# Four-layer transformer block on one core: order of the third layer's projections, weight loads on another queue, and accumulation banks by use

## The chip, the cores and the metric

One core of one Trainium2 chip runs the whole program. The metric is device time in microseconds (us), the median of three runs. The core's engines work in parallel, each through its own instruction stream in order: TensorE (PE; its weight loads are shown as PEld), VectorE (DVE), ScalarE (ACT), GpSimd (POOL) and SyncE (SP), which here only issues transfers. DMA transfers are issued by SP and by POOL, each in its own order, and are carried by 16 DMA engines. Matrix products land in PSUM, which here is cut into three score buffers of two banks each and two further banks for everything else. SBUF holds all other tiles.

## What is computed

x has the shape 4 x 1024 x 256 (batch, rows, width), float32. Four layers follow each other, each with a residual:

```python
x = x + attn_a(layernorm(x))     # layer 1: 16 heads of 64, full softmax attention
x = x + ffn(layernorm(x))        # layer 2: 256 -> 1024 -> 256, exact gelu
x = x + attn_b(layernorm(x))     # layer 3: the same attention from low-rank projections
x = x + ffn(layernorm(x))        # layer 4: the same weights as layer 2

# attn_b, with its own normalization inside (scale and bias), b, s, d = x.shape
c_q, c_kv = h @ w_down_q.T, h @ w_down_kv.T            # 256 -> 128
q, k, v   = c_q @ w_up_q.T, c_kv @ w_up_k.T, c_kv @ w_up_v.T
q, k      = rope(q), rope(k)                           # even and odd features rotated
attn      = softmax(q @ k.T / 8)
out       = (attn @ v) @ w_out.T + x_normalized        # attn_b adds its own input
```

## The kernel before

The order of every engine's work is written out by hand; no scheduler changes it. Instructions of one engine run in the order in which the program issues them, and a semaphore makes an instruction wait for what it reads or overwrites.

**Attention (`attention`, L163 to L323).** Heads are taken in pairs, because two heads of 64 fill the 128 rows of TensorE: 4 batches x 8 pairs = 32 pairs. A pair has eight steps, one for each 128 query rows: 256 steps in each of layers 1 and 3. Two steps are one block `h`. In step s the loop `steps_with` (L294) issues, in this order:

1. `invert(s)`: reciprocal of the softmax sums (DVE), copied into the probabilities (ACT).
2. `scores(s + 1)`: eight matmul records `sc` (L214), and `exponentials(s + 1, 0)`: the negated row maximum `nmax` (DVE, L224) and the exponential (ACT, L225) of the first head.
3. In even steps `send(s // 2 - 1)` on POOL (five of 16 transfers of a block, L261) and `project` of an earlier block: output projection `po` (PE), copy `got` (ACT, L290), residual add (POOL, L292).
4. `weigh(h, part)`: half of the weighted sums `av` (PE) of block h = (s - 4) // 2, first half in even steps, second in odd. The accumulation stays open from the even to the odd step.
5. `exponentials(s + 1, 1)` for the second head.
6. In odd steps `divide(h)`: `av` times the inverted sums gives `oT` (DVE, L275).
7. `turn(s)`: transposes 32 x 32 squares of the probabilities (DVE, L244).
8. In odd steps `send(s // 2)` on SP (the other eleven transfers): squares from `T` to `pT`, which completes the transpose. `weigh` reads `pT` about two and a half steps later.
9. The `pieces` that are due in step s: projections of the next pair and preparations of the next batch.

**The pieces.** In layer 1 (`pair_a`, L484) the next pair's `pq` (keys, queries: `qk`) and `pv` (`values`) come in odd steps. In layer 3 (`pair_b`, L578) too: `qk` in steps 7, 1, 3 and 5 (counted within a pair), `values` in steps 5 and 7, always at the end of the step. `qk` ends in a scaled copy (ACT) and two transfers on POOL that swap neighbouring features (`turned`, L598); `rotate`, one step later, is three POOL operations (L603 to L605). The three weights `w` of a pair come by POOL transfers in step 4 (L584), the output weight `wo` in step 7 (L190). A new batch in layer 3 (`batch_b`, L536) needs four transposes `tr` with their copies (`turned`, in odd steps), and four down projections `pc` (`down`, L562), two in each of two odd steps.

**Banks.** `ps_mm` (L52) has two buffers that are handed out in turn to `tr`, `pq`, `pv`, `pc`, `av` and `po`.

**Layer 2 and 4 (`ffn_between`, L393).** Blocks of 512 rows; layer 3's first batch and first pair are prepared inside layer 2.

**Start (L635 to L640).** Measuring and normalizing batch 0, its transposes, all four `pq` and four `pv` of the first pair, then the first scores.

Of the kernel before, what the change touches and what calls it, by code (L numbers as in the profile page):

```python
# [9 lines left out]
F32 = mybir.dt.float32  # L10
AF = mybir.ActivationFunctionType
ALU = mybir.AluOpType
# [19 lines left out]
SENT = NG * HB * NK * SQ  # L32
POOL_DMA = 5
EPS = 1e-5


@with_exitstack
def hybrid_block_kernel(
# [10 lines left out]
    small = ctx.enter_context(tc.tile_pool(name="small", bufs=6))  # L49

    ps_sc = ctx.enter_context(tc.tile_pool(name="ps_sc", bufs=3, space=PSUM))
    ps_mm = ctx.enter_context(tc.tile_pool(name="ps_mm", bufs=2, space=PSUM))  # L52


    pool = lambda name, bufs: ctx.enter_context(tc.tile_pool(name=name, bufs=bufs))
# [83 lines left out]

    def transposed(dst, src, c, affine=None):  # L140

        tr = ps_mm.tile([P, TQ, P], F32, tag="mm", name="tr")
        for t in range(TQ):
            nc.tensor.transpose(tr[:, t, :], src[:, t, ts(c, P)], ident)
        trf = tr.rearrange("p t q -> p (t q)")
        if affine is None:
            nc.scalar.copy(dst[:, c, :], trf)  # L147
        else:
            nc.scalar.activation(
                dst[:, c, :], trf, AF.Identity,  # L150
                scale=affine[0][:, c : c + 1], bias=affine[1][:, c : c + 1],
            )
# [7 lines left out]
                    start=(first and i == 0), stop=(last and i == len(parts) - 1),  # L160
                )

    def attention(prep_batch, prep_pair, wo):  # L163

# [20 lines left out]

        def load_out(g):
            wos[g] = wop.tile([P, D], F32, tag="wo", name="wo")
            nc.gpsimd.dma_start(wos[g], wo[ts(pairs[g][1], P), :])  # L190

        for g, (b, pr) in enumerate(pairs):
            for k, f in prep_batch(b) if pr == 0 else ():
# [69 lines left out]
        def weigh(h, part):  # L263
            v = tiles[HB * h // NT]["v"]()
            if part == 0:
                av[h] = ps_mm.tile([P, HB * P], F32, tag="mm", name="av")
            half = range(part * NT // 2, (part + 1) * NT // 2)
            paired(
                av[h], [(v[:, k], [pT[h][:, :, :, j * NT + k, :] for j in range(2)]) for k in half],
                first=(part == 0), last=(part == 1),  # L270
            )

        def divide(h):
            oT[h] = otp.tile([P, HB * P], F32, tag="oT", name="oT")
            nc.vector.tensor_tensor(  # L275
                oT[h].rearrange("p (q a i) -> p a q i", a=NG, i=SQ),
                av.pop(h).rearrange("p (a q i) -> p a q i", a=NG, i=SQ),
                pT.pop(h)[:, :, :, 2 * NT, :],
                op=ALU.mult,
            )  # L280

        def project(h):
            g, t0 = divmod(HB * h, NT)
            b, pr = pairs[g]
            po = ps_mm.tile([P, HB, D], F32, tag="mm", name="po")
            for t in range(HB):
                paired(po[:, t, :], [(oT[h][:, ts(t, P)], [wos[g]] * 2)])
            oT.pop(h)
            got = tmp.tile([P, HB, D], F32, tag="tmp", name="got")
            nc.scalar.copy(got, po)  # L290
            xd = xs[b][:, t0 : t0 + HB, :]
            nc.gpsimd.tensor_add(xd, xd, got)  # L292

        def steps_with(others):  # L294
            for k, f in others:
                pieces.setdefault(k, []).append(f)
            for s in range(-1, n + LAG + 1):
                h, part = divmod(s - LAG, HB)
                ahead = 0 <= s + 1 < n
                if 0 <= s < n:  # L300
                    invert(s)
                if ahead:
                    scores(s + 1)
                    exponentials(s + 1, 0)
                if part == 0 and 0 <= s // HB - 1 < n // HB:
                    send(s // HB - 1, nc.gpsimd, squares[len(squares) - POOL_DMA :])
                    T.pop(s // HB - 1)
                if part == 0 and 0 <= h - 1 < n // HB:
                    project(h - 1)
# [35 lines left out]
    def ffn(rows, store):  # L345
# [29 lines left out]
        def down(n, t):  # L375
            b, qb = blocks[n]
            if t % 2 == 0:
                po[n] = ps_mm.tile([P, 2, D], F32, tag="mm", name="po")
# [72 lines left out]
    def layer_a():  # L451
# [5 lines left out]
        def batch_a(b):  # L457
            work = []
            for qb in range(NQB):
                k = {}  # L460

                def straight(t, b=b, k=k, qb=qb):
                    if t == 0 and b == 0:
                        for i in range(TQ):
                            rows.measure(qb, i)
                        rows.finish[qb]()
                    if t == 0:
                        k["xn"] = xnp.tile([P, TQ, D], F32, tag="xn", name="xn")
                    standardize(
                        k["xn"][:, t, :], xs[b][:, qb * TQ + t, :],  # L470
                        *rows.factors(NQB * b + qb, t)[:2],
                    )

                def turned(c, b=b, k=k, qb=qb):
                    if c == 0:
                        p, tag = ((lowp, "low"), (highp, "high"))[qb]
                        hTs[b, qb] = p.tile([P, NC, QB], F32, tag=tag, name="hT")
                    transposed(hTs[b, qb], k["xn"], c)

                work += [(10 * qb + t, lambda t=t, f=straight: f(t)) for t in range(TQ)]  # L480
                work += [(10 * qb + 5 + 2 * c, lambda c=c, f=turned: f(c)) for c in range(NC)]
            return work

        def pair_a(b, pr):  # L484
# [9 lines left out]
            def qk(i, qb):  # L494
                name = ("qT", "kT")[i]
                if qb == 0:
                    made[name] = qkp.tile([P, S], F32, tag=name, name=name)
                pq = ps_mm.tile([P, QB], F32, tag="mm", name="pq")
# [9 lines left out]
            def values(m):  # L508
                if m == 0:
                    made["v"] = vp.tile([P, NT, P], F32, tag="v", name="v")  # L510
                pv = ps_mm.tile([P, 2, P], F32, tag="mm", name="pv")
# [12 lines left out]

        later = [(4 + i, lambda i=i: rows.measure(2 + i // TQ, i % TQ)) for i in range(6 * TQ)]
        later += [(4 + 6 * TQ, lambda: rows.finish[2]())]
        first, steps = attention(batch_a, pair_a, wo_a)
        return first, lambda others: steps(later + others)


    def layer_b(rows):
# [4 lines left out]
        def batch_b(b):  # L536
            work = []
            for qb in range(NQB):
# [23 lines left out]
                def down(i, k=k, qb=qb):  # L562
                    if qb == 0:
                        cs[b, i] = highp.tile([P, NC, QB], F32, tag="high", name=f"c{i}").rearrange(
                            "p c q -> p (c q)"
                        )
                    pc = ps_mm.tile([P, QB], F32, tag="mm", name="pc")
# [4 lines left out]
                work += [(10 * qb + t + 2, lambda t=t, f=second: f(t)) for t in range(TQ)]  # L572
                work += [(10 * qb + 7 + 2 * c, lambda c=c, f=turned: f(c)) for c in range(NC)]

                work += [(3 * NT + 1 - 2 * i, lambda i=i, f=down: f(i)) for i in range(2)]
            return work

        def pair_b(b, pr):  # L578
            made = {}

            def load():
                w = made["w"] = wp.tile([P, 3, NC, P], F32, tag="w", name="w")[:, :, 0, :]
                for i, up in enumerate((wuq, wuk, wuv)):
                    nc.gpsimd.dma_start(w[:, i], up[:, ts(pr, P)])  # L584

            def qk(i, qb):

                pq = ps_mm.tile([P, QB], F32, tag="mm", name="pq")
# [18 lines left out]
            def values(qb):  # L607
                if qb == 0:
                    made["v"] = vp.tile([P, NT, P], F32, tag="v", name="v")
                pv = ps_mm.tile([P, TQ, P], F32, tag="mm", name="pv")  # L610
# [90 lines left out]
```

## Time and profile before

| | us |
|---|---|
| median of three runs (lowest, highest) | 3390.42 (3387.98, 3392.9) |
| the profiled execution | 3386.3 |
| its span, first to last instruction | 3384.5 |
| first transpose to last transpose of layer 1 | 1435.6 |
| first transpose to last transpose of layer 3 | 1400.7 |

Busy time of the engines over the span: TensorE 3253.2 (96%), VectorE 2593.1 (77%), ScalarE 1902.1 (56%), GpSimd 1800.8 (53%). The span in 40 slices of 85 us each, one digit a slice (tenths busy; 9 is 90% or more), shows the four layers: slices 1 to 17 are layer 1, 18 to 20 layer 2, 21 to 37 layer 3, the rest layer 4.

```
PE   7999999999999999999999999999999999999999
DVE  6988888888888888951059998898889989999200
POOL 3333334343333333330258887888788978886200
DMA  7788788788887888840038888888888888888200
```

The transfers of `pT` are 2816 on SP (median 4.2 us from issue to landing) and 1280 on POOL (4.7 us), 136 KB each. The swapped copies `turned` are 256 on POOL, 128 KB each (median 2.7 and 3.0 us). In the views, `128*64` ahead of a shape is the part of TensorE's array that is used, and `x8` at a line's end counts merged instructions.

### The profile page before, as it was taken

To read this page: it belongs to the slowest core of one execution; us is meant where nothing else is said; L and a number is where in the kernel's file an instruction comes from. 1 tells how busy PE (TensorE), PEld (TensorE's weight loads), DVE (VectorE), ACT (ScalarE), POOL (GpSimd) and SP (SyncE) were. 2 spreads that over 40 slices of the span, in tenths; PEclk is the share of its full clock that TensorE was granted. 3 is DMA by queue.
4 is the path that set the end of the run, shared out by engine and by line. 5 is a ranking of instruction groups with operands and counts; after the bars stand their busy time and mean duration, and the time that the engine had idled before them with its cause. 6 is when DMAs were issued, how large, how long until landed. Compare 5 with 4: busy or idle time off the path is not lost.

```text
span 3384.5 us, 60980 instructions
## 1 busy us (share of the span) xinstructions
PE 3253.2 (96%) x20864; PEld 1679.4 (50%) x20864; DVE 2593.1 (77%) x2638; ACT 1902.1 (56%) x3667; POOL 1800.8 (53%) x2546
## 2 busy tenths in 40 slices
PE   7999999999999999999999999999999999999999
PEld 3445444544454444456554444444444444444566
DVE  6988888888888888951059998898889989999200
ACT  5566556655565555542445665566656655655332
POOL 3333334343333343330258887888788978886200
PEclk9999999999999999999999999999999999999999
DMA  7788788888887888840038888888888888888200
GB/s 211 204 210 208 205 214 212 211 208 214 210 210 206 214 214 210 210 115 3 6 105 233 227 239 226 237 246 231 224 236 243 242 225 239 243 235 228 61 19 19
DMA packets 229585, 647.36 MB, mean 191 GB/s; under 512 B 74304, under 2 KB 82496, under 8 KB 229280
## 3 DMA queue, kind: packets, MB, share of 16 engines
q1 hardware_dynamic: 143696, 400.74, 46.2%
q0 software_dynamic: 85584, 242.74, 25.2%
q8 instruction: 170, 2.79, 0.4%
q14 instruction: 135, 1.11, 0.1%
HBM read 35.00 MB, written 4.19 MB: 12 GB/s over the span
## 4 chain that ended last, share of the span: by engine, by line
PE 67%; DVE 11%; SPq 8%; DMA 6%; issue 4%; ACT 3%; POOL 1%; DVEq 0%; POOLq 0%; ACTq 0%
PE sc L214 19%; PE av L158 18%; SPq L261 8%; PE pq L158 8%; PE po L380 7%; PE ph L369 6%; DVE nmax L224 5%; DVE T L244 5%; DMA pT<-T 5%; PE po L158 4%; PE pv L158 4%; ACT p L225 1%; PE pc L158 1%; DMA turned<-qT 1%; DVE oT L275 1%
## 5 line engine op out<-in xcount | busy, mean ns | idle before, releaser
L225 ACT ACTIVATE p<-sc,nmax 128x1024 f32<-128x1024 f32 x1024 | 1143.8, 1117 | 729.5 <-DVE nmax L224 729.5
L224 DVE TENSOR_REDUCE nmax<-sc 128x1 f32<-128x1024 f32 x1024 | 1201.9, 1215 | 325.5 <-PE sc L214 324.9
L244 DVE STREAM_TRANSPOSE T<-p 128x2176 f32<-128x2176 f32 x512 | 1246.3, 2434 | 11.1 <-ACT p L233 3.9
L158 PE MATMUL av<-pT,v 128*64 128x256 f32 x8192 | 994.7, 385 | 79.4 <-DMA pT<-T 56.9
L214 PE MATMUL sc<-kT,qT 64*128 64x512 f32 x4096 | 1033.0, 617 | 7.2 <-ACT p L225 7.2
L261 POOL DMA_DIRECT2D pT<-T x1280 | 625.8, 496 | 777.9 <-issue 268.7
L158 PEld LDWEIGHTS av<-pT,v 128*64 128x64 f32 x8192 | 579.5, 137 | 542.9 <-issue 273.3
L214 PEld LDWEIGHTS sc<-kT,qT 64*128 64x128 f32 x4096 | 366.8, 187 | 483.9 <-issue 352.5
L292 POOL TENSOR_TENSOR x<-x,got 128x512 f32<-128x512 f32 x256 | 326.8, 1276 | 224.7 <-ACT got L290 220.4
L233 ACT COPY p<-total 128x128 f32<-128x128 f32 x512 | 152.0, 297 | 312.5 <-DVE total L232 312.4
L387 DVE TENSOR_TENSOR x<-x,po 128x512 f32<-128x512 f32 x32 | 21.9, 685 | 363.4 <-PE po L380 363.4
L158 PE MATMUL po<-wo,oT 128*64 128x256 f32 x2048 | 277.7, 392 | 0.4 <-DVE oT L275 0.4
L373 ACT ACTIVATE gT<-ph,b_sb 128x512 f32<-128x512 f32 x128 | 87.4, 685 | 305.4 <-PE ph L369 305.3
L158 PE MATMUL pq<-hT,w 128*64 128x512 f32 x1024 | 247.0, 605 | 5.1 <-DVE oT L275 4.0
L158 PEld LDWEIGHTS po<-wo,oT 128*64 128x64 f32 x2048 | 124.3, 136 | 230.2 <-issue 129.5
L380 PE MATMUL po<-w_sb,gT 128*128 128x256 f32 x1024 | 226.0, 381 | 6.2 <-ACT hT L147 6.2
L369 PE MATMUL ph<-hT,w_sb 128*128 128x512 f32 x512 | 228.9, 601 | 0.2 <-ACT hT L147 0.2
L380 PEld LDWEIGHTS po<-w_sb,gT 128*128 128x128 f32 x1024 | 193.5, 190 | 38.4 <-ACT hT L147 9.0
L225 ACT ACTIVATION_READ_ACCUMULATOR p<-sc,nmax 128x1 f32 x1024 | 201.4, 197 | 0.0
L355 POOL TENSOR_TENSOR x<-x,b_sb 128x256 f32<-128x256 f32 x64 | 44.5, 727 | 276.4 <-ACT xn L138 276.4
L604 POOL TENSOR_TENSOR turned<-turned,sin_sb 128x512 f32<-128x512 f32 x128 | 162.3, 1268 | 0.0
L369 PEld LDWEIGHTS ph<-hT,w_sb 128*128 128x128 f32 x512 | 97.0, 192 | 117.1 <-issue 111.3
(88 smaller groups left out, 2188.8 us busy)
## 6 DMA issues: line engine op xcount, KB each, us to landing
pT<-T SPq DMA_DIRECT2D x2816, 136.0 KB, 4.2
pT<-T POOLq DMA_DIRECT2D x1280, 136.0 KB, 4.7
turned<-kT POOLq DMA_DIRECT2D x128, 128.0 KB, 2.7
turned<-qT POOLq DMA_DIRECT2D x128, 128.0 KB, 3.0
w<-in_wqkv_a POOLq DMA_DIRECT2D x96, 128.0 KB, 4.9
wo<-in_wo_a POOLq DMA_DIRECT2D x32, 128.0 KB, 4.4
wo<-in_wo_b POOLq DMA_DIRECT2D x32, 128.0 KB, 3.4
out<-x SPq DMA_DIRECT2D x16, 256.0 KB, 2.1
```

The costliest lines, as they stand in the source:

```text
L158: nc.tensor.matmul(out[ts(j, DH)], lhsT[:, ts(j, DH)], rhs[j], start=(first and i == 0), stop=(last and i == len(parts) - 1),)
L214: nc.tensor.matmul(sc[s, j][:, ts(m, 512)], qT()[rows, ts(qs, P)], kT()[rows, ts(m, 512)], start=True, stop=True,)
L224: nc.vector.tensor_reduce(nmax, sc[s, j], AX.X, ALU.max, negate=True)
L225: nc.scalar.activation(probs[s][:, ts(j, NT)].rearrange("p k c i -> p (k c i)"), sc.pop((s, j)), AF.Exp, bias=nmax, accum_out=total[s][:, ...
L233: nc.scalar.copy(probs[s][:, 2 * NT].rearrange("p (j c) i -> p j (c i)", j=2), t.unsqueeze(2).to_broadcast([P, 2, DH]),)
L244: nc.vector.transpose(T[h][:, :, q, :, :].rearrange("p c k i -> p k c i"), probs.pop(s))
L261: engine.dma_start(pT[h][ts(c, SQ), a], T[h][ts(a, SQ), c])
L292: nc.gpsimd.tensor_add(xd, xd, got)
L369: nc.tensor.matmul(ph, w1_sb[:, c, ts(f, P)], hT[n][:, c, :], start=(c == 0), stop=(c == NC - 1),)
L373: nc.scalar.activation(gT[n][:, f, :], ph, AF.Gelu, bias=b1_sb[:, f : f + 1])
L380: nc.tensor.matmul(po[n][:, t % 2, :], gT[n][:, f, ts(t, P)], w2_sb[:, f, :], start=(f == 0), stop=(f == NF - 1),)
L604: nc.gpsimd.tensor_mul(turned, turned, sin_sb[:, ts(qb, QB)])
```

## The change

1. **Banks.** `ps_mm` becomes two named buffers. `group` hands out the one that was not used last; while the weighted sums `av` are open (`keep=True` until `divide` is issued) everything else gets the other one.
2. **Layer 3, order within a step.** `turn(s)` is issued ahead of `divide(h)` (`divide_first=False`); layer 1 keeps its order.
3. **Layer 3, pieces.** `qk` is due half a step earlier (`EARLY`): in the same odd steps, but ahead of `weigh`, that is between the scores and the second half of `av`. `values` move from steps 5 and 7 to the ends of steps 4 and 6. The four `down` of a batch move from two odd steps to four even ones (k = 22, 24, 26, 28: steps 6, 0, 2, 4), keys' and values' first.
4. **Layer 3, loads.** `w` and `wo` are issued on SP instead of POOL, at the same places of the program: `w` at the end of step 4, `wo` at the end of step 7, behind the block's eleven sends.
5. **Start of layer 1.** Both row blocks are measured by separate calls; the second block's rows are scaled on VectorE (`tensor_scalar`) instead of ScalarE; an exponential of one column (`ready`) is issued ahead of the transposes' copies; key projection of the first half comes ahead of the second block's transposes; one query projection and the four `values` are issued in steps -1 to 1.

```diff
+EARLY = 0.5
...
-    ps_mm = ctx.enter_context(tc.tile_pool(name="ps_mm", bufs=2, space=PSUM))
+    ps_mm = ctx.enter_context(tc.tile_pool(name="ps_mm", bufs=1, space=PSUM))
+    bank = {"last": 1, "kept": None}
+    def group(shape, name, keep=False):
+        i = 1 - (bank["last"] if bank["kept"] is None else bank["kept"])
+        bank["last"] = i
+        if keep:
+            bank["kept"] = i
+        return ps_mm.tile(shape, F32, tag=f"m{i}", name=name)
...
-        tr = ps_mm.tile([P, TQ, P], F32, tag="mm", name="tr")
+        tr = group([P, TQ, P], "tr")
...
-    def attention(prep_batch, prep_pair, wo):
+    def attention(prep_batch, prep_pair, wo, loader, divide_first):
...
-            nc.gpsimd.dma_start(wos[g], wo[ts(pairs[g][1], P), :])
+            loader.dma_start(wos[g], wo[ts(pairs[g][1], P), :])
...
-                av[h] = ps_mm.tile([P, HB * P], F32, tag="mm", name="av")
+                av[h] = group([P, HB * P], "av", keep=True)
...
             oT[h] = otp.tile([P, HB * P], F32, tag="oT", name="oT")
+            bank["kept"] = None
...
+                for f in pieces.get(s - EARLY, ()):
+                    f()
                 if 0 <= h < n // HB:
                     weigh(h, part)
                 if ahead:
                     exponentials(s + 1, 1)
+                if not divide_first and 0 <= s < n:
+                    turn(s)
                 if part == 1 and 0 <= h < n // HB:
                     divide(h)
-                if 0 <= s < n:
+                if divide_first and 0 <= s < n:
                     turn(s)
...
-                    if t == 0 and b == 0:
-                        for i in range(TQ):
-                            rows.measure(qb, i)
-                        rows.finish[qb]()
...
+                    if b == 0 and qb == 1:
+                        nc.vector.tensor_scalar(dst, src, rstd, shift, op0=ALU.mult, op1=ALU.add)
+                    else:
+                        standardize(dst, src, shift, rstd)
...
-        first, steps = attention(batch_a, pair_a, wo_a)
+        first, steps = attention(batch_a, pair_a, wo_a, nc.gpsimd, divide_first=True)
+        loads, xn, pair = first[:2], first[2:14], first[14:]
+        def measured(qb):
+            for t in range(TQ):
+                rows.measure(qb, t)
+            rows.finish[qb]()
+        def ready():
+            nc.scalar.activation(small.tile([P, 1], F32, tag="nmax", name="ready"), eps, AF.Exp)
+        first = loads + [lambda: measured(0)] + xn[:4] + [lambda: measured(1), ready] + xn[4:6] + pair[:1]
+        first += xn[6:] + pair[1:3]
+        later += [((-1, 0, 0, 1, 1)[i], f) for i, f in enumerate(pair[3:])]
...
-                work += [(3 * NT + 1 - 2 * i, lambda i=i, f=down: f(i)) for i in range(2)]
+                work += [(3 * NT - 2 + 4 * (1 - i) + 2 * qb, lambda i=i, f=down: f(i)) for i in (1, 0)]
...
-                    nc.gpsimd.dma_start(w[:, i], up[:, ts(pr, P)])
+                    nc.sync.dma_start(w[:, i], up[:, ts(pr, P)])
...
-                    work += [(k, lambda i=i, qb=qb: qk(i, qb))]
+                    work += [(k - EARLY, lambda i=i, qb=qb: qk(i, qb))]
                     work += [(k + 1, lambda i=i, qb=qb: rotate(i, qb))]
-            work += [(5 + 2 * qb, lambda qb=qb: values(qb)) for qb in range(NQB)]
+            work += [(4 + 2 * qb, lambda qb=qb: values(qb)) for qb in range(NQB)]
...
-        return attention(batch_b, pair_b, wo_b)
+        return attention(batch_b, pair_b, wo_b, nc.sync, divide_first=False)
```

The other uses of `ps_mm` (`po`, `pq`, `pv`, `pc`) take their tile from `group` in the same way.

More of the change, by code (lines that the diff above doesn't have):

```diff
@@ L284, in project @@
             b, pr = pairs[g]
-            po = ps_mm.tile([P, HB, D], F32, tag="mm", name="po")
+            po = group([P, HB, D], "po")
             for t in range(HB):
@@ L377, in down @@
             if t % 2 == 0:
-                po[n] = ps_mm.tile([P, 2, D], F32, tag="mm", name="po")
+                po[n] = group([P, 2, D], "po")
             for f in range(NF):
@@ L462, in straight @@
                 def straight(t, b=b, k=k, qb=qb):
-                    if t == 0 and b == 0:
-                        for i in range(TQ):
-                            rows.measure(qb, i)
-                        rows.finish[qb]()
                     if t == 0:
                         k["xn"] = xnp.tile([P, TQ, D], F32, tag="xn", name="xn")
[L469 to L472, printed above, removed]
+                    dst, src = k["xn"][:, t, :], xs[b][:, qb * TQ + t, :]
+                    shift, rstd = rows.factors(NQB * b + qb, t)[:2]
+                    if b == 0 and qb == 1:
+                        nc.vector.tensor_scalar(dst, src, rstd, shift, op0=ALU.mult, op1=ALU.add)
+                    else:
+                        standardize(dst, src, shift, rstd)
                 def turned(c, b=b, k=k, qb=qb):
@@ L497, in qk @@
                     made[name] = qkp.tile([P, S], F32, tag=name, name=name)
-                pq = ps_mm.tile([P, QB], F32, tag="mm", name="pq")
+                pq = group([P, QB], "pq")
                 paired(pq, [
@@ L510, in values @@
                     made["v"] = vp.tile([P, NT, P], F32, tag="v", name="v")
-                pv = ps_mm.tile([P, 2, P], F32, tag="mm", name="pv")
+                pv = group([P, 2, P], "pv")
                 for t in range(2):
@@ L566, in down @@
                         )
-                    pc = ps_mm.tile([P, QB], F32, tag="mm", name="pc")
+                    pc = group([P, QB], "pc")
                     paired(pc, [(wd_sb[:, i, c, :], [k["hT"][:, c, :]] * 2) for c in range(NC)])
@@ L583, in load @@
                 for i, up in enumerate((wuq, wuk, wuv)):
-                    nc.gpsimd.dma_start(w[:, i], up[:, ts(pr, P)])
+                    nc.sync.dma_start(w[:, i], up[:, ts(pr, P)])
             def qk(i, qb):
-                pq = ps_mm.tile([P, QB], F32, tag="mm", name="pq")
+                pq = group([P, QB], "pq")
                 paired(pq, [(made["w"][:, i, :], [cs[b, i][:, ts(qb, QB)]] * 2)])
@@ L609, in values @@
                     made["v"] = vp.tile([P, NT, P], F32, tag="v", name="v")
-                pv = ps_mm.tile([P, TQ, P], F32, tag="mm", name="pv")
+                pv = group([P, TQ, P], "pv")
                 for t in range(TQ):
```

## The prediction

> **What bounds the kernel now.** I read the busy windows first, then who waits, then the timeline of two steps, then the chain. The windows compare layer 1 (first row) with layer 3 (second); columns are length, busy of PE, PEld, DVE, ACT and POOL, granted clock, DMA share, GB/s.
>
> ```profile
> 400.00:1450.00 1050.00, 1046.89 (x7506) 522.54 (x7504) 915.62 (x859) 625.31 (x1238) 407.15 (x648) 1.00 0.81 211
> 1900.00:2700.00 800.00, 753.27 (x5064) 368.58 (x5062) 712.82 (x662) 503.27 (x978) 675.85 (x896) 0.99 0.86 235
> ```
>
> In layer 1 TensorE is busy 99.7%: only the start can change there. In layer 3 it is idle 5.8%, and VectorE, the DMA engines and GpSimd stand at 89%, 86% and 84%. The list of waits says what TensorE lacks: transposed weights. In layer 3 alone I find 72 of 119 blocks (a block h is two steps) in which `av` starts late, 85 us together, 0.7 a block.
>
> ```profile
> DVE nmax L224 <- PE sc L214: 324.9, 271, 17.1
> PE av L158 <- DMA pT<-T: 56.9, 49, 2.6
> ```
>
> Two steps of layer 3 without such a wait (start, length, engine, line):
>
> ```profile
> 2413.28 2.44 DVE L244 STREAM_TRANSPOSE T<-p 128x2176 f32<-128x2176 f32 x1
> ...
> 2413.64 1.99 PE L214 MATMUL sc<-kT,qT 64*128 64x512 f32 x8
> ...
> 2415.56 1.95 PE L158 MATMUL av<-pT,v 128*64 128x256 f32 x16
> ...
> 2415.68 2.34 DVE L224 TENSOR_REDUCE nmax<-sc 128x1 f32<-128x1024 f32 x2
> ...
> 2417.34 1.03 PE L158 MATMUL pq<-c,w 128*64 128x512 f32 x4
> ...
> 2417.93 0.42 DVE L275 TENSOR_TENSOR oT<-av,pT 128x256 f32<-128x256 f32 x1
> ...
> 2418.27 2.43 DVE L244 STREAM_TRANSPOSE T<-p 128x2176 f32<-128x2176 f32 x1
> ...
> 2420.22 1.08 PE L158 MATMUL po<-wo,oT 128*64 128x256 f32 x8
> ```
>
> Start to start TensorE's pieces are sc 1.92, av 1.78 to 1.83, pq 0.96, po 0.91; pv is 1.09 elsewhere. VectorE needs 9.64 for the two steps (2413.28 to the next such transpose at 2422.92). The divide stands ahead of the transpose and costs it 0.34.
>
> The chain of waits shows the path that sets the pace:
>
> ```profile
> 2849.25 0.51 SPq L261
> ...
> 2857.34 3.35 DMA pT<-T
> ...
> 2861.25 1.95 PE av L158 x16
> 2863.20 1.97 PE sc L214 x8
> ```
>
> Eleven sends on SP, the last landing, then av. Over blocks 4 to 123 the last send lands 11.97 us after the transpose that it carries (10.4 to 14.5), and av, where it waits, starts 0.5 later: 12.47. From av to the end of the transpose two blocks on: av 1.86, sc 1.99, maxima and their start 2.30, divide 0.33 net, transpose 2.44, together 8.92. So two blocks cost 12.47 + 8.92 = 21.39, four blocks (a pair of heads) 42.8; pairs without down projections measure 43.1. TensorE's own way, av 1.86 + sc 1.92 + av 1.88 + pq 0.86 + sc 1.92 + po 0.91 = 9.35 a block (10.46 with pv), is hidden behind 10.70. **Layer 3 runs at the pace of the sends.**
>
> **The change, part by part.**
>
> *Start.* Before, scores begin at 27.85. One pq (2.03 there: 8.10 for four) and four pv (3.7) move behind the first scores. New order: ScalarE's four standardizations end at 10.0, then root 0.3, table load and `ready` 1.5 (the load was hidden at 28.36), two hT copies to 13.1; pq to 15.1; second transposes 2.7 to 17.8, copies to 18.5; two pq to about 22.6; the copy of qT 0.6; scores at 23.2: 4.7 sooner. VectorE's four standardizations (bn_stats of the same size: 0.39 each) end by 12.7, hidden. The moved matmuls fall into steps where TensorE waits (1.70 and 1.44 before scores); some may not fit. I take -4, bounds -6 and -2. Measuring both blocks costs VectorE what it cost before.
>
> *Divide behind the transpose.* The sends leave 0.33 earlier. But project waits for the divide: from the end of scores, divide ends at 2.30 + 2.44 + 0.33 = 5.07, while TensorE is ready after pq, av and scores at 4.6. A new loop: av 1.86, sc 1.99, 5.07, wake-up 0.05, po 0.91 = 9.88 a block.
>
> *Keys and queries ahead of av, values in even steps.* pq on ScalarE stands between two exponentials: the second ends 0.6 later, at 4.4 after the scores, still ahead of the reciprocal at 5.0. pv (1.11 with its switch) now stands after the first half of av and ahead of the scores, so in two blocks of four it is inside both loops, where before it was hidden behind the sends.
> Send loop now: 12.47 + 8.59 = 21.06, or 22.17 with pv. Project loop over two pv blocks 2 x 10.99 = 21.98, over two others 19.76. Four blocks: 22.17 + 21.06 = 43.23 if the sends take as long, +0.45; if they land 0.3 sooner, 21.98 + 20.76 = 42.74, -0.04.
>
> *Sends, loads, turned copies.* SP gains three w loads and one wo load per pair, POOL loses four (0.55 to 0.60 each, 2.3 a pair, and the sends, turned copies and rotations queued behind them). SP is idle 1.9 a block between its last issue and the next transpose (median); three loads at 0.59 fill it, on a way without slack. An SP issue here takes 0.5 to 1.6, so the loads cost 1.5 to 4.8: nearest is the plain 0.59, hidden. Turned copies are issued some 1 us earlier relative to the sends, which frees part of the stretch, 2.5 to 9.5 after a transpose, in which the packets keep the engines 95% busy. Bounds from rows: blocks 121 to 127, with neither loads nor turned copies, land after 11.15, 0.8 sooner (4 blocks 42.24, -0.54); SP late by 0.3, the other way, 43.83 (+1.05). I take 0.15 sooner: +0.2 x 30 pairs = +6, bounds -16 and +32.
>
> *Banks.* While av is held all else shares the other bank; after the divide is queued the next group takes av's bank. In layer 3 that next group is the batch's `tr` (four odd steps per batch, three batches: 12), as pq has already gone. So `tr` waits for the divide, now behind the transpose: TensorE is through with av 2.65 after the scores, the divide ends at 5.07: 2.4 idle, with the next scores, project and av queued behind it, and VectorE waiting for those scores. Part is hidden where av would have waited for sends (0.4 of the 0.7 above): 12 x 2.0 = +24, bounds +9 and +30. Before, the divide ended at 2.6, and `tr` cost its 0.69 alone.
>
> Such idle also drops the clock. After a stall of 2.58 at 1831.7 the granted clock was 0.57 over four microseconds; after 2.91 at 1907.7 it stayed full:
>
> ```profile
> 1834.00:1838.00 4.00, 3.70 (x18) 2.09 (x20) 2.98 (x4) 1.54 (x4) 3.98 (x8) 0.57 0.95 244
> ...
> 1911.00:1915.00 4.00, 4.00 (x26) 1.71 (x24) 3.31 (x4) 2.34 (x6) 1.44 (x3) 1.00 0.23 41
> ```
>
> Half rate for 3.4 us costs 1.7; at about every second stall of this size, 12 x 0.5 x 1.7 = 10, less some cover: +8, bounds 0 and +20. The Trainium skill, "TensorE: Matmul & The Clock Gate", Part 1, says that the clock halves after at least one idle window of about 3.4 us: by that a 2.4 us wait is free, and the sum would be 8 lower. The 2.58 us stall speaks against it here, so the row decides.
>
> *Downs in four steps.* Before, two at once (3.43) at the end of two odd steps; pairs 6/7, 14/15, 22/23 exceed 43.1 by 21.1 in all, 7.0 a batch. Now one (1.72) in each of four even steps, all inside the project loop: 6.9, and in two of them it waits for ScalarE's copy of pv in the same bank (0.65 each). 8.2 less what the sends cover (1.1): 0 net, bounds -10 and +6.
>
> Sum: -4 + 6 + 24 + 8 + 0 = +34. On the profiled execution's 3386.3 that is 3420; the median of the runs shown lies 4.1 above that execution, so a median may come at 3424. I say 3420.
>
> **The rivals.**
> 1. *Faster: the sends really shorten.* With loads off POOL and turned copies out of the way they land 0.8 sooner (-16), start -6, downs -6, and the tr waits cost their lower 9 with the clock full: 3386 - 19 = 3367; with tr at 16, 3374. For it: POOL at 84%, and where its sends start late (22 blocks) the last lands 1.2 later. Against it: POOL's own sends land 1 to 7 us before av needs them; SP's land last. It decides from 0.7 us sooner on if tr costs 16 and the clock holds (-0.4 a pair x 30 = -12), from 1.2 on with my values.
> 2. *SP becomes worse.* If the loads go like SP's slow issues (1.5 each, 4.5 in all), 4.5 less SP's idle 1.9 leaves the next block's sends 2.6 late, once a pair; with 0.6 of cover that is 2.0 x 30 = +60 on top: 3480. For it: SP's idle time is all used. Against it: the slow issues come while its own sends pile up, three to five into a block, not at its end.
> 3. *Layer 3 nets nothing*: tr's waits fall where sends are late anyway, and only the start is left: 3382.
>
> **How the numbers follow.** Forecast 0.6, SP worse 0.1, faster 0.2, nothing 0.1. A measurement of this kernel can tell 0.2%, 6.8 us. Faster: 0.19 of rival 1 and half of rival 3, 0.24. Same: the rest of these and 0.03 of the forecast, 0.09. Slower 0.57 and rival 2, 0.67. The likeliest case's own range is 3395 to 3448; to hold 8 in 10 it must reach into the first rival: 3374 to 3452.
>
> **What would show it.** Scores at 23 in the first microseconds. In layer 3: `po` waiting for `oT` about 0.5 in most blocks; `tr` waiting for `oT` 12 times, 2 us and more, with half clock after some; less wait of av for pT than 85; POOL at 80%. If `tr`'s wait is absent or the sends land a microsecond sooner, the forecast is wrong; if SP's first send starts late after the loads, rival 2 is right.

## The result, and the profile after

The changed kernel takes 3447.3 us (median of 6 runs, 3442.36 to 3452.05), the kernel before 3389.2 beside it (6 runs, 3372.31 to 3392.9). The ratio is 1.0178, 95% interval 1.0161 to 1.0195: slower by 58 us, where +34 was forecast.

| us | before | after |
|---|---|---|
| span of the profiled execution | 3384.5 | 3444.1 |
| first scores | 27.85 | 22.30 |
| last transpose of layer 1 | 1471.5 | 1467.7 |
| first to last transpose of layer 3 | 1400.7 | 1459.0 |
| last transpose of layer 3 to the end | 248.7 | 253.4 |
| a pair of heads in layer 3 (mean of 15 pairs) | 43.09 | 43.97 |

The 15 pairs are 8 to 11, 16 to 19 and 24 to 30, in which no `tr` and no down projection of a new batch falls; they are called plain pairs below. The whole loss lies in layer 3. The start of layer 1 is won as planned; in the timeline of TensorE (start, length, engine, line, operation, in brackets the idle time before it and what ended it) three of the four `pq` (8 records each) now stand ahead of the first scores, where before all four stood there with the `pv`:

```profile
12.55 3.68 PE L169 MATMUL pq<-hT,w 128*64 128x512 f32 x8 [0.92 <-ACT hT L158]
16.16 1.66 PE L155 MATMUL tr<-ident,xn 128*128 128x128 f32 x8
17.95 3.65 PE L169 MATMUL pq<-hT,w 128*64 128x512 f32 x16
22.30 1.99 PE L225 MATMUL sc<-kT,qT 64*128 64x512 f32 x8 [0.70 <-ACT qT L518]
```

The busy windows over the same stretches as before (layer 1, layer 3; busy of PE, PEld, DVE, ACT, POOL, then clock, DMA share, GB/s):

```profile
400.00:1450.00 1050.00, 1045.38 (x7483) 520.63 (x7480) 914.65 (x858) 624.23 (x1237) 406.61 (x649) 1.00 0.81 210
1900.00:2700.00 800.00, 723.39 (x4794) 347.95 (x4792) 673.70 (x627) 475.69 (x924) 606.54 (x783) 0.98 0.83 224
```

Layer 1 is as it was. In layer 3 everything has become less busy: TensorE 90% instead of 94%, VectorE 84 instead of 89, GpSimd 76 instead of 84, the DMA engines 83 instead of 86. Nothing took the place of a bound; the engines now wait for each other. The list of waits says where (total, times, longest):

```profile
DVE nmax L235 <- PE sc L225: 376.9, 240, 11.3
...
PE po L169 <- DVE oT L287: 51.2, 112, 0.6
PE tr L155 <- DVE oT L287: 34.2, 15, 2.6
PE av L169 <- DMA pT<-T: 31.1, 26, 3.3
...
PE av L169 <- DMA wo<-in_wo_b: 7.1, 9, 1.5
```

`av` waits for transposed weights 31 us instead of 57. In its place `po` waits for the divide 112 times and `tr` 15 times (12 of them at the three new batches of layer 3, 28.4 us, 2.37 each; the other three at the layer's end), and VectorE waits 377 instead of 325 us for scores. The timeline of one block with `pv`, from the scores of an odd step on, shows the order that does it:

```profile
2179.11 1.99 PE L225 MATMUL sc<-kT,qT 64*128 64x512 f32 x8
...
2183.40 2.44 DVE L255 STREAM_TRANSPOSE T<-p 128x2176 f32<-128x2176 f32 x1
2183.76 1.99 PE L225 MATMUL sc<-kT,qT 64*128 64x512 f32 x8
...
2185.76 0.39 DVE L287 TENSOR_TENSOR oT<-av,pT 128x256 f32<-128x256 f32 x1
...
2186.17 15.86 SPq L272 DMA_DIRECT2D pT<-T  x16
2186.20 1.08 PE L169 MATMUL po<-wo,oT 128*64 128x256 f32 x8 [0.45 <-DVE oT L287]
2187.14 1.95 PE L169 MATMUL av<-pT,v 128*64 128x256 f32 x16
...
2189.10 1.09 PE L169 MATMUL pv<-w,c 128*64 128x128 f32 x16
2190.13 1.99 PE L225 MATMUL sc<-kT,qT 64*128 64x512 f32 x8
...
2197.22 1.08 PE L169 MATMUL po<-wo,oT 128*64 128x256 f32 x8 [0.45 <-DVE oT L287]
```

From one `po` to the next it is 11.02 us, and each time TensorE stands 0.45 for the divide, which ends (2186.15) 5.1 after the scores of its own step (2181.10); the scores at 2183.76 belong to the next step. The line of SP shows something else: the sends do not start when the transpose ends (2185.84) but when the divide ends (2186.15). The chain of waits now runs through divide, projection and `pv`; before, it went from the sends to `av`:

```profile
2160.47 0.58 SPq L201
...
2161.30 3.44 DMA pT<-T
...
2164.74 3.42 PE av L169 x16
...
2183.49 2.35 DVE T L255
2185.84 0.32 DVE oT L287
...
2186.20 1.08 PE po L169 x8
2187.28 1.81 PE av L169 x16
...
2189.10 1.09 PE pv L169 x16
2190.20 1.97 PE sc L225 x8
```

The first lines are a block in which the sends are still late (the load of `wo`, SPq L201, stands among them): both loops are in the chain, by turns. The `av` of 3.42 instead of 1.9 ran at half clock (the trace's clock records have 0.5 from 2164.4 on, for 3.41). At a `tr` the same can be seen in the timeline, and in windows around it:

```profile
2341.35 0.68 PE L155 MATMUL tr<-ident,x 128*128 128x128 f32 x4 [2.37 <-DVE oT L287]
2341.96 3.61 PE L225 MATMUL sc<-kT,qT 64*128 64x512 f32 x8
```

```profile
2337.00:2341.00 4.00, 1.99 (x18) 1.01 (x14) 4.00 (x4) 2.79 (x5) 3.73 (x5) 1.00 0.58 164
...
2341.80:2345.20 3.40, 3.40 (x10) 1.19 (x8) 0.00 (x0) 0.96 (x2) 2.22 (x5) 0.51 0.76 213
```

2.37 us of waiting for the divide, then scores of 3.61 instead of 1.99 at a granted clock of 0.51, while VectorE does nothing at all (0.00). By the trace's clock records layer 3 has 14 such drops, 58.0 us at half clock, against 6 and 20.5 before; 7 of the 12 waits of `tr` are followed by one. That and TensorE's idle time in layer 3, 132 instead of 88 us, roughly account for the loss: 44 more idle and, at half rate, 19 more by the clock, an estimate of 63 against the 58 by which the layer grew. Part of the difference in clock is chance: e3, an experiment below whose layer 3 has the order of the kernel before, has 41.0 us at half clock. Over whole runs the mean granted clock is 0.989 to 0.991 in the changed kernel and 0.991 to 0.996 in 35 runs of the kernel before (mean 0.994); 0.004 of 3440 us is 14 us, an estimate of what the clock can account for.

Summed over TensorE's gaps (my own reckoning from its records, gaps under 0.02 left out), a plain pair divides like this; the other rows are experiments told below:

| us per plain pair | busy | waits for the divide (`po`, in e5 `pq`, in before, e3 and f1 `pv` and `pq`) | `av` waits, mostly for transfers | `pv` waits for `got` | sum |
|---|---|---|---|---|---|
| before | 40.33 | 0.1 | 2.64 | 0 | 43.1 |
| e3, order of before | 40.78 | 0.1 | 2.80 | 0 | 43.7 |
| after | 40.35 | 1.82 | 1.61 | 0.19 | 44.0 |
| e1, order of after but for `tr` | 40.65 | 1.82 | 1.68 | 0.12 | 44.3 |
| f1, before with half the values | 39.79 | 0.1 | 3.29 | 0 | 43.2 |
| f2, after with half the values | 39.79 | 1.83 | 1.95 | 0.08 | 43.7 |
| e5, values in even steps alone | 40.52 | 1.73 | 1.89 | 0.57 | 44.7 |

Each row is one execution. Rows of the same order differ by 0.3 to 0.6 in the sum, mostly in the busy time, which holds the half clock too; the waits repeat better.

### The profile page after: what moved, and what is told of

Its sections match the earlier page's. It is cut to its first block, busy times and chain, and to the rows that moved or that the text cites. A ratio compares the mean times of both kernels' runs of the same rounds, so it can differ in the third digit from the quotient of the medians.

```text
span 3444.1 us, 60724 instructions
## 1 busy us (share of the span) xinstructions
PE 3266.0 (95%) x20864; PEld 1675.3 (49%) x20864; DVE 2591.8 (75%) x2642; ACT 1900.9 (55%) x3664; POOL 1734.8 (50%) x2418
## 4 chain that ended last, share of the span: by engine, by line
PE 63%; DVE 17%; SPq 6%; issue 6%; DMA 5%; ACT 3%; DVEq 0%; POOL 0%; ACTq 0%
PE sc L225 19%; PE av L169 15%; DVE T L255 8%; DVE nmax L235 7%; PE pq L169 7%; PE po L396 7%; PE ph L385 6%; SPq L272 6%; PE pv L169 5%; PE po L169 4%; DMA pT<-T 3%; PE pc L169 1%; ACT p L236 1%; DMA wo<-in_wo_b 1%; DVE oT L287 1%
## 5 line engine op out<-in xcount | busy, mean ns | idle before, releaser
L255 DVE STREAM_TRANSPOSE T<-p 128x2176 f32<-128x2176 f32 x512 | 1246.1, 2434 | 13.8 <-DMA pT<-T 5.1
L169 PE MATMUL av<-pT,v 128*64 128x256 f32 x8192 | 989.4, 384 | 42.1 <-DMA pT<-T 31.1
L169 PEld LDWEIGHTS av<-pT,v 128*64 128x64 f32 x8192 | 588.3, 138 | 480.2 <-issue 217.1
```

What stands on the lines that cost most here:

```text
L169: nc.tensor.matmul(out[ts(j, DH)], lhsT[:, ts(j, DH)], rhs[j], start=(first and i == 0), stop=(last and i == len(parts) - 1),)
L255: nc.vector.transpose(T[h][:, :, q, :, :].rearrange("p c k i -> p k c i"), probs.pop(s))
```

## The experiments

All ratios are to the kernel before, run beside them on the same chip. First the parts of the changed kernel are undone one by one (e1, e2, e4), then it is built up from the kernel before (e3, e5, e7); e9, f1 and f2 try single claims.

### e1: the transposes in another bank

```diff
-    def group(shape, name, keep=False):
-        i = 1 - (bank["last"] if bank["kept"] is None else bank["kept"])
+    def group(shape, name, keep=False, same=False):
+        i = bank["last"] if same else 1 - (bank["last"] if bank["kept"] is None else bank["kept"])
...
-                    transposed(k["hT"], k["x1"], c, affine=(lns_sb, lnb_sb))
+                    transposed(k["hT"], k["x1"], c, affine=(lns_sb, lnb_sb), same=b > 0)
```

> The changed kernel, but the transposes tr of layer 3's batches 1 to 3 take the bank that the projection pq has just left, not the one of the weighted sums; so they wait for ScalarE's copy of pq (at about 3.1 us after the scores) and not for the divide (5.07). Theory: the 12 waits of tr for the divide cost their 28 us and the half clock that follows them. Expected: the 12 waits fall from 2.4 us to under 0.6 each, half-clock windows in layer 3 from 13 to 8 or fewer, the time falls by 25 to 35 us, to 3412 to 3422. Rival: the waits lie where the sends are late anyway; then av's wait for pT takes their place and the time falls by under 10 us.

Measured: 3420.68 (before 3382.97), ratio 1.0091 (1.0057 to 1.0125); 29 us less than the changed kernel by the ratios, 27 by the medians. In its list of waits:

```profile
PE po L169 <- DVE oT L287: 51.2, 112, 0.6
...
PE tr L155 <- DVE oT L287: 5.8, 3, 2.6
...
PE tr L155 <- ACT kT L625: 2.7, 9, 0.3
```

The 12 waits of the new batches are gone (the three that are left belong to the layer's end); `tr` waits 0.3 for a copy instead. Of the pairs that carry `tr`, 4, 5 and 6 go from 50.4, 45.7 and 50.3 to 46.1, 42.7 and 48.0; all nine together (12 to 14 and 20 to 22 too) are 29.4 us shorter, and the plain pairs are not (4.5 longer). The choice of a bank for four small transposes a batch costs half of the loss. The drops of the clock fall from 14 to 9 (13 to 8, as expected, without the one at the layer's end), 41.0 us at half clock, so not all of them come from `tr`.

### e2: the divide ahead of the transpose again

```diff
-        return attention(batch_b, pair_b, wo_b, nc.sync, divide_first=False)
+        return attention(batch_b, pair_b, wo_b, nc.sync, divide_first=True)
```

> The changed kernel with layer 3's divide ahead of the transpose again; all else as changed. Theory (order of divide and transpose costs by the project loop and by tr): po's waits for oT (49 us in 109) and tr's (28 us in 12) go, but the divide now waits 0.4 us for av, which comes behind pq, and carries the transpose and the sends with it. Expected: send loop 9.25 + 12.2 = 21.4 for two blocks, 22.5 with the values, so no gain from the loop, and about 30 us from tr: 3410 to 3425. Rival (values in even steps are the loop's cost): the same here, as they stay; what tells them apart is the pattern of a pair: if the two blocks with values still take 11.0 and the others fall from 9.83 to under 9.7, the values bind and not the divide.

Measured: 3461.85, ratio 1.0216 (1.0184 to 1.0247). A miss: slower than the changed kernel by some 13 us, where the intervals of the two ratios still overlap, and not faster by 22 to 37. Its waits:

```profile
PE av L169 <- DMA pT<-T: 46.4, 30, 4.0
DVE oT L287 <- PE av L169: 43.9, 116, 0.4
PE pv L169 <- ACT got L302: 33.9, 41, 1.1
PE av L169 <- DMA wo<-in_wo_b: 25.4, 16, 2.3
```

`po` no longer waits, and `tr` 0.53 instead of 2.37. But with `pq` ahead of the second half of `av`, `av` ends so late that the divide, and VectorE behind it, waits 0.4 in nearly every block (116 times); the transpose ends 5.56 after the scores instead of 4.74, the sends start later, and `av` waits for them and for the loads again. The pattern that was to tell the rivals apart fits neither: from `po` to `po`, blocks with values take 11.5 instead of 11.0 and the one without 10.0 instead of 9.83. With keys and queries ahead, the divide is better behind the transpose; the two edits belong together.

### e4: the loads back on POOL

```diff
-                    nc.sync.dma_start(w[:, i], up[:, ts(pr, P)])
+                    nc.gpsimd.dma_start(w[:, i], up[:, ts(pr, P)])
...
-        return attention(batch_b, pair_b, wo_b, nc.sync, divide_first=False)
+        return attention(batch_b, pair_b, wo_b, nc.gpsimd, divide_first=False)
```

> The changed kernel with layer 3's weights loaded by POOL again. Theory: the loads on SP lie in SP's idle time and cost nothing; the sends land as soon, av's waits for pT stay near 35 us, and POOL is busier by 0.57 us a load: within 8 us of the changed kernel, 3440 to 3455. Rival (loads on SP delay the sends of the next block): the time falls by 15 us or more. Rival (POOL's relief was worth something): it grows by 10 us or more, and POOL's sends start late as before (22 of 128 blocks over 2 us; 5 in the changed kernel).

Measured: 3450.5, ratio 1.0183 (1.0149 to 1.0217): the same as the changed kernel. The waits of `av` for `wo` are gone, and others of the same size stand in their place. Which queue carries the loads decides nothing here. Nor is it the loads that made POOL's sends punctual: they start more than 2 us after the transpose in 6 of blocks 4 to 123 here, in 5 in the changed kernel and in 22 in the kernel before.

### e3: the start and the banks alone

The kernel before with the new start of layer 1 and `group`; layer 3 keeps its order, divide, downs and loads. The diff is against the changed kernel.

```diff
-                work += [(3 * NT - 2 + 4 * (1 - i) + 2 * qb, lambda i=i, f=down: f(i)) for i in (1, 0)]
+                work += [(3 * NT + 1 - 2 * i, lambda i=i, f=down: f(i)) for i in range(2)]
...
-                    nc.sync.dma_start(w[:, i], up[:, ts(pr, P)])
+                    nc.gpsimd.dma_start(w[:, i], up[:, ts(pr, P)])
...
-                    work += [(k - EARLY, lambda i=i, qb=qb: qk(i, qb))]
+                    work += [(k, lambda i=i, qb=qb: qk(i, qb))]
...
-            work += [(4 + 2 * qb, lambda qb=qb: values(qb)) for qb in range(NQB)]
+            work += [(5 + 2 * qb, lambda qb=qb: values(qb)) for qb in range(NQB)]
...
-        return attention(batch_b, pair_b, wo_b, nc.sync, divide_first=False)
+        return attention(batch_b, pair_b, wo_b, nc.gpsimd, divide_first=True)
```

> The kernel before with only the start of layer 1 and the banks by use; layer 3's order, loads and down projections as before. Theory: layer 1 ends 3.8 us sooner as in the changed kernel and layer 3 is as before, for with no group between the two halves of av the banks go in turn as they did: 3385, between 3380 and 3389. Rival (banks by use cost something by themselves): layer 3 grows, 3395 or more.

Measured: 3383.1, ratio 0.9994 (0.9977 to 1.0011). Layer 1 ends 3.6 us sooner (1467.9), but a gain of 4 is too small to be told from none. By themselves the banks cost nothing that shows.

### e5 and e7: values in even steps, then downs in four steps

e5 is e3 with one line changed, e7 is e5 with another:

```diff
-            work += [(5 + 2 * qb, lambda qb=qb: values(qb)) for qb in range(NQB)]
+            work += [(4 + 2 * qb, lambda qb=qb: values(qb)) for qb in range(NQB)]
```

```diff
-                work += [(3 * NT + 1 - 2 * i, lambda i=i, f=down: f(i)) for i in range(2)]
+                work += [(3 * NT - 2 + 4 * (1 - i) + 2 * qb, lambda i=i, f=down: f(i)) for i in (1, 0)]
```

> Start and banks as in the changed kernel; of layer 3's changes only the values, moved from the ends of steps 5 and 7 to the ends of steps 4 and 6. Keys and queries, divide, loads and downs as before. Theory: pv (1.1 us) comes between av's first half and the next scores, so it is on the way from the landing of the sends to the transpose two blocks on: 42.8 for four blocks becomes 43.9, 0.8 to 1.1 us a pair over 30 pairs, 25 to 35 us slower than the kernel with the start alone: 3408 to 3420. Rival: pv fills time in which TensorE waits for the sends anyway; then the time is within 8 us of the kernel before.

> As the kernel with values in even steps, and the four down projections of a batch in four even steps. Theory: each pc (1.72) moves from the end of an odd step into the same way as pv, where it is not covered, but two at once no longer follow each other: 7 us a batch before and after, so within 8 us of the kernel with values in even steps alone. Rival (spreading them is a gain): 10 us or more faster than that kernel.

Measured: e5 3425.06 (before 3388.87), ratio 1.0108 (1.0086 to 1.013), +36; e7 3441.25, 1.0155 (1.0137 to 1.0173), another +16. e5 lies a little above its range, and its list of waits shows a part that was not in the theory:

```profile
PE pq L169 <- DVE oT L287: 58.0, 65, 3.2
...
PE av L169 <- DMA pT<-T: 40.6, 37, 2.5
...
PE pv L169 <- ACT got L302: 15.7, 40, 0.9
```

In the even step `pv` takes the spare bank; `pq`, next in line in the odd step, then gets the bank of `av` and waits 0.9 for the divide. Blocks with `pv` take 6.36 + 5.44 = 11.8 us (from transpose to transpose) instead of 4.98 + 5.45 = 10.4. So the move of the values alone costs more than half of what the whole change costs, by the loop that it lengthens and by the bank that it shifts; how much of it is the bank was not separated.

e7 was a miss: within 8 us was expected. Pairs 7, 15 and 23, the last of each batch, take 51.7 us in e7 against 46.0 in e5 (the pairs before them, 6, 14 and 22, win back 0.8 to 2.0), always with the same steps: the downs land in even steps, two of them in those that also have `pv` (8.99 instead of 6.37). Only in company with keys ahead, where the steps are 8.65 and 6.88, does the move come out even.

Put in a row, the kernels build up the change. Steps of ratio, in us of the kernel before: start and banks (e3) -2; values in even steps (e5) +39; downs in four steps (e7) +16; keys and queries ahead of `av`, with the loads on SP (e2) +21; divide behind the transpose (the changed kernel) -13. Together they are the +60 of the ratio; `tr` in another bank (e1) would take 29 off. What a step costs depends on those before it, so e1's 29 and e5's 39 are not parts to be added.

### e9: one more send on POOL, loads on SP

The kernel before, to see what the sends are worth: SP issues ten instead of eleven of a block's sends and carries the loads.

```diff
-POOL_DMA = 5
+POOL_DMA = 6
...
-                    nc.gpsimd.dma_start(w[:, i], up[:, ts(pr, P)])
+                    nc.sync.dma_start(w[:, i], up[:, ts(pr, P)])
...
-        return attention(batch_b, pair_b, wo_b)
+        return attention(batch_b, pair_b, wo_b, nc.sync)
```

> The kernel before with layer 3's weights loaded by SP and six of a block's sixteen sends on POOL instead of five, in both attention layers. Theory (SP's eleven sends set layer 3's pace by their issue): the last of ten sends is issued 0.6 to 0.75 sooner and lands 0.3 to 0.6 sooner, POOL's six are through at 3.5 instead of 2.9 after the transpose; four blocks 42.2 instead of 42.8: 10 to 20 us faster than before, 3363 to 3375. Rival (the sixteen DMA engines, 95% busy from 2.5 to 9.5 us after a transpose, set it): the last landing stays at 11.7 to 12.0, the time within 6 us of the kernel before.

Measured: 3404.15, ratio 1.005 (1.0033 to 1.0067), +15: outside both ranges. SP's last send is issued 7.76 after the transpose instead of 8.36, yet the last of its sends lands 12.07 after it, instead of 11.97; POOL's land 9.88 instead of 9.11. So issuing the last send sooner did not make it land sooner. `av` now also waits for `wo`:

```profile
PE av L158 <- DMA pT<-T: 51.6, 34, 3.2
...
PE av L158 <- DMA wo<-in_wo_b: 13.7, 13, 1.6
```

The wait for `pT` is 5 us shorter than in the kernel before, that for `wo` is new; what the rest of the 15 us is was not taken apart.

### f1 and f2: half of the values left out

The sharpest test of the claim on steps: the same work is taken out of an odd step (f1, the kernel before) and out of an even one (f2, the changed kernel). The two kernels differ in more than this step; e5 with half of its values, which beside e3 would differ in it alone, was not run.

```diff
                 if qb == 0:
                     made["v"] = vp.tile([P, NT, P], F32, tag="v", name="v")
+                if qb == 1:
+                    nc.scalar.copy(made["v"][:, ts(1, TQ)], made["v"][:, ts(0, TQ)])
+                    return
```

> The kernel before, with the second half of a pair's value projection in layer 3 left out: those four pairs of matmuls (pv, 1.1 us, step 7) are not made, and ScalarE copies the first half's values in their place, a copy of the same size. 30 pairs have it, 33 us of TensorE in all. Theory (in the odd step a projection lies beside a wait of TensorE for the transposed weights): nearly nothing is won, 0 to 10 us under the kernel before, 3379 to 3389. Rival (TensorE's own time counts wherever it stands): 20 us and more, 3369 or less.

> The changed kernel with the same half of the value projection left out (step 6). Theory (in the even step the projection lies inside the loop from the scores through divide and output projection to the next scores, and nothing hides it): 17 to 33 us are won, 3414 to 3430, with the ordinary pairs near 43.2 instead of 43.97. Rival (the loss of the changed kernel comes from the sends and from TensorE's clock, not from this matmul): 0 to 10 us, 3437 to 3447, as in the kernel before.

Measured: f1 3386.51 (before 3384.42), ratio 1.001 (0.9995 to 1.0025): 33 us of matmuls are gone and nothing is won. f2 3427.77, ratio 1.0129 (1.0114 to 1.0144): 17 us less than the changed kernel by the ratios, 20 by the medians, at the low end of the range; plain pairs 43.66, not 43.2. The waits of f1, then of f2:

```profile
PE av L158 <- DMA pT<-T: 66.6, 52, 2.7
```

```profile
PE po L169 <- DVE oT L287: 51.6, 112, 0.6
PE av L169 <- DMA pT<-T: 42.7, 39, 3.1
```

In f1 the wait for the sends grows from 56.9 to 66.6, in the plain pairs from 2.64 to 3.29 a pair: what is taken out in the odd step comes back as waiting. A smaller part goes with the clock: its mean over f1's runs is 0.992, beside 0.994 in the kernel before, some 8 us by estimate. In f2 the wait grows too (31.1 to 42.7), so of 33 us only half is won: the changed kernel has two loops of nearly the same length, and shortening one shows the other. The traced execution of f2 also had more half clock (81.9 us in layer 3 instead of 58.0; 10 of its 12 `tr` waits were followed by a drop), so its plain pairs show less of the gain than the medians.

## Why the prediction was right, and where its sum was off

*Direction and mechanism* held: the loop through divide and projection, the bank of `tr` and the clock are what the runs show. The term that was mis-sized is that of the two loops. The size was off by 24 of 58 us, and 3447 lies at the slow end of the likeliest case's own range, 3395 to 3448.

*Start, -4:* measured 3.8 sooner at the end of layer 1; in e3, with the banks, too small to tell.

*"The sends leave 0.33 earlier": wrong.* SP's first send comes 0.34 after the transpose, before 0.08. `pT` has two buffers; the divide of block h - 2 still reads the one that the sends of block h overwrite, so a divide behind the transpose holds back the sends by its own length. The prediction followed the divide's reading of `av` and forgot its read of `pT`. Counted from the scores, the transpose ends 0.33 sooner (4.74 instead of 5.07) and the first send leaves only 0.06 sooner. The last landing is 0.63 sooner all the same (16.41 instead of 17.04 after the scores), where the prediction's two terms give 0.48; with the loads back on POOL (e4) it is 16.57, and what else makes it is not shown. A third `pT` buffer was not tried.

*Loops, sends, loads, +6, bounds -16 to +32:* measured 0.87 a plain pair in the two traces, some 26 us over 30 pairs; from the medians, 58 less the other terms below, it is 29. The sizes of the loops were right: 9.83 and 11.02 a block, forecast 9.88 and 10.99; the last landing came 0.30 after the transpose sooner, forecast 0.15. The error is in how they were put together: of two loops of equal length only the longer was counted. The table of plain pairs shows what happens instead: `po` waits 1.82 a pair for the divide, and only 1.03 of it comes out of the 2.64 that `av` waited before. The reading that fits, argued and not tested by itself: blocks in which the sends are late (landings 10.4 to 14.5 us after the transpose before, 10.5 to 13.8 after) still pay in full, and those in which they are not now pay at `po`; the mean of the longer of two loops with such a spread is more than the longer of their means. f2 fits that: a loop shortened by 1.1 a pair won some 0.6, its 17 to 20 us over 30 pairs. Which edit lengthened the loops, the row of experiments tells in part: the values first, then keys and queries ahead.

*`pv` in both loops:* confirmed in kind by f1 and f2 (nothing against 17 us), and by e5, which adds a bank's share.

*Waits of `tr`, +24 within 9 to 30, and half clock, +8:* 28.4 us in 12 waits, 7 drops of the clock behind them, 1.7 us each; e1 gives both together as 27 to 29, forecast 32. The waits and those drops add up to 40, less 2.7 that `tr` still waits in e1, so some 8 to 11 us were covered or came back elsewhere; where is not shown. The 2.4 us waits did halve the clock: the row of the trace was the better guide, and the Trainium skill's rule of one idle window of about 3.4 us ("TensorE: Matmul & The Clock Gate", Part 1) does not agree with these runs, in which the 3.41 us before a drop were up to half busy (last section). The other 7 of the 14 drops lie elsewhere in layer 3, where the kernel before has its 6; what they cost is inside the terms of the pairs.

*Loads on SP, hidden:* right, by e4. Rival 2 is out: SP's first send of a block comes at most 0.85 after the transpose (blocks 4 to 123), not 2.6.

*Downs, 0 net:* right in the whole (some 7 a batch before and after), but by company alone: e7 shows +16 without keys ahead, and no run undoes the move in the changed kernel.

*Not costed:* the end of layer 3, +4.7; its last transposes wait for the same late divide, and the clock is at half for 6.8 us there, before for 3.4.

Sum of what was measured (28 for `tr` and its clock, from e1): -4 + 26 + 28 + 0 + 5 = +55, against +58. Rival 1 asked for landings 0.8 sooner after the transpose; they came 0.30 sooner, and 0.47 in e2, where the divide does not hold the sends back. Rival 3 (the waits of `tr` lie where sends are late anyway) failed at e1. What stays open is how the spread of the sends makes the 26 to 29 us, what sets the last landing, and the rest of e9.

## What to carry to other kernels

When two loops run at nearly the same pace, cost an edit to one of them with the spread of the other, not with the larger mean; a table of one engine's waits per period shows how much of a new wait is paid by an old one. Work of a bound engine is free only in the part of the period where that engine waits already: the same matmul cost nothing in the odd step and about half its length in the even one. An instruction that is moved delays everyone who overwrites what it reads, and every group that takes its bank next; look for both before the matmuls are counted.

## What was unexpected in the hardware

Waits of TensorE of 2.37 us were enough to have the clock granted at half (0.51) for 3.4 us, but not always: 7 of 12 equal waits did it in the changed kernel, 10 of 12 in f2, 6 of 12 in e4. The clock records of the eleven traces show what decides. From 60 us on, all their stretches of half clock begin on a grid of 3.413 us, fixed within an execution, and last one or two of its cells. Where TensorE was busy less than 0.41 of a cell at full clock, the next cell was at half in 90 of 90 cases; over 0.56, in none of 10458; between them, in 34 of 118. Two of the `tr` waits, each in a cell (length, busy of PE, PEld, DVE, ACT and POOL, clock, DMA share, GB/s), the first followed by the drop at 2341.80:

```profile
2338.39:2341.80 3.41, 1.04 (x10) 0.56 (x6) 2.97 (x4) 1.94 (x5) 2.56 (x4) 1.00 0.43 147
2386.20:2389.61 3.41, 2.29 (x12) 1.11 (x12) 1.13 (x3) 1.06 (x4) 2.48 (x6) 1.00 0.86 255
```

The first wait lies wholly in its cell and leaves it busy 0.31, as at all seven that were followed by a drop; the second lies across a border, 0.63 and 0.68 busy on its two sides, and at all five without a drop the emptier cell was busy 0.51 or more. So which of several equal waits costs the clock depends on where the grid happens to fall. It is the same in the kernel before: the wait of 2.58 that ended at 1834.3 left its cell busy 0.26, that of 2.91 fell across a border, 0.52 and 0.63.

The landing of a block's last send did not follow its issue: ten sends on SP instead of eleven were issued 0.6 sooner and landed no sooner (12.07 against 11.97 us after the transpose).
